# The last image's convolution in a two-layer vision model: where its second batches accumulate in PSUM

## The chip, the cores and the metric

The kernel runs on one core of a Trainium2 chip. The metric is device time in microseconds of one launch: the median of the runs. Three runs of the kernel before gave 10369.3, 10372.5 and 10379.58 us.

The core has TensorE (PE, matrix products into the accumulation memory PSUM), VectorE (DVE), ScalarE (ACT), GpSimd (POOL) and SyncE (SP, which here starts the DMA transfers). PSUM has 8 banks; a bank holds 512 float32 numbers in each of 128 partitions.

## The reference, cut to what matters

Two layers work on four images of 64 x 64 pixels with 128 channels. Layer 0 is attention and a recurrent network; layer 1 is a selective scan and a mixture of experts. The change is in the first part of the selective scan:

```
xz = jnp.einsum('bhwc,ec->bhwe', x, in_proj_w)
xin, z = jnp.split(xz, 2, axis=-1)
xc = jnp.transpose(xin, (0, 3, 1, 2))
xc = lax.conv_general_dilated(xc, conv_w, (1, 1), [(1, 1), (1, 1)],
                              feature_group_count=d, ...)
xc = jax.nn.silu(xc + conv_b[None, :, None, None])
x0 = xc.reshape(B, d, L)
x1 = jnp.transpose(xc, (0, 1, 3, 2)).reshape(B, d, L)
```

So each image is normalised, projected to 256 channels `xin` and 256 gates `z`, and each of the 256 channels is convolved with its own 3 x 3 filter. The result passes through silu and is kept in two orders, by rows (`x0`) and by columns (`x1`), for the scans that follow.

## The kernel before

The program runs attention, then the recurrent network, then `selective_scan`, then `experts`. `selective_scan` calls three functions one after the other: `scan_inputs` (what is shown above, L824), `scans` (L951) and `scan_outputs`. Results pass between them in DRAM. `scans` can begin only when the memory that `scan_inputs` holds has come free.

Inside `scan_inputs` three generators each take an image `b`:
- `centred(b)` (L855) loads the image, subtracts the mean and sums the squares in a PSUM tile with the tag `norm`, which has one bank (L121 writes it, L132 reads it).
- `projected(b)` (L871) scales the image (L145, L148) and, for each of 8 chunks of 512 pixels, makes four products `in_ps` (L880). Each takes one of three banks with the tag `mm`. DVE copies the first two to `xin` (L884), and ACT writes the other two to `z` through silu (L886).
- `convolved(b)` (L890) takes the two halves `h` of 128 channels, and in each half two batches of four chunks, `c0 = 0` and `c0 = 4`. So an image has four batches.

A batch is one PSUM tile with the tag `conv`, of four banks and with one buffer (L895). With `mm` and `norm` this makes 3 + 1 + 4 = 8 banks, all there are. The filter is carried out on PE as nine taps, each a product with a 32 x 32 diagonal matrix. The loops are: tap `n`, chunk `i` of the batch, strip `r` of 32 channels (L896 to L904). Strip `r` of the channels goes to bank `r`, and chunk `i` to partitions `32*i` to `32*i + 31`. That is 9 x 4 x 4 = 144 products, which the profile shows as 288 records, two for each.

Then ACT empties the tile with 16 activations of 32 partitions by 512 numbers (L914), bank by bank, into `u`. After both batches of a half, POOL copies `u` into the order by columns (`uc`, L922), and SP stores both (L927). The first load of `scans` is a constant, `w_x`, at L159.

The driver (L935 to L947) runs `convolved(b)` and, after each of its batches, two steps of `projected(b + 1)` and of `centred(b + 2)`. For the last image, `b = 3`, there is nothing of those two left. The order of instructions in an engine's queue in this stage isn't written out by hand: a scheduler sets it when the program is built, starting from the order of the program and from when tiles come free. In `scans` the order is written out by hand.

Of the kernel before, what the change touches and what calls it, by code (L numbers as in the profile page):

```python
# [19 lines left out]
F32 = mybir.dt.float32  # L20
# [6 lines left out]
P = 128  # L27
B, HW, C = 4, 64, 128
L = HW * HW
CH = 512  # L30
# [18 lines left out]
def chunk(c):  # L49
    return slice(c * CH, (c + 1) * CH)  # L50
# [100 lines left out]
def constant(nc, pool, value, name, shape=(P, 1)):  # L151
    t = pool.tile(list(shape), F32, name=name, tag=name)
    nc.vector.memset(t, value)
    return t


def loaded(nc, pool, src, name):
    t = pool.tile(list(src.shape), F32, name=name, tag=name)
    nc.sync.dma_start(t, src)  # L159
    return t  # L160
# [662 lines left out]
@with_exitstack  # L823
def scan_inputs(ctx, tc, a, x2, us, gates):  # L824

    nc = tc.nc
    cst = ctx.enter_context(tc.tile_pool(name="si_c", bufs=1))
    big = ctx.enter_context(tc.tile_pool(name="si_b", bufs=1))
    work = ctx.enter_context(tc.tile_pool(name="si_w", bufs=2))
    ps = ctx.enter_context(tc.tile_pool(name="si_p", bufs=3, space=PSUM))  # L830

    ident = cst.tile([P, P], F32, name="ident")
    make_identity(nc, ident)
    norms = Norms(nc, cst, ident, C, banks=3)
    eps6 = constant(nc, cst, 1e-6, "eps6")
    w_in = loaded(nc, cst, a["w_in"], "w_in")
    w_conv = loaded(nc, cst, a["w_conv"], "w_conv")
    zeros = constant(nc, cst, 0.0, "zeros", (P, LP - L))
    taps = [(0, 0)] + [
        (dy, dx) for dy in (-1, 0, 1) for dx in (-1, 0, 1) if (dy, dx) != (0, 0)  # L840
    ]


    ident32 = cst.tile([P, 32], F32, name="ident32")
    b_conv = cst.tile([P, ND, 4], F32, name="b_conv")
    for i in range(4):
        rows = slice(32 * i, 32 * i + 32)
        nc.vector.tensor_copy(ident32[rows], ident[rows, rows])
        nc.sync.dma_start(b_conv[rows], a["b_conv"].rearrange("(r j) h -> j h r", j=32))
    diag = cst.tile([P, ND, 9, 32], F32, name="diag")  # L850
    for h in range(ND):
        for n in range(9):
            nc.vector.tensor_scalar_mul(diag[:, h, n, :], ident32, w_conv[:, h, n : n + 1])

    def centred(b):  # L855
        ln = big.tile([P, L], F32, tag="ln", name=f"ln_{b}", bufs=2)
        var = norms.begin(ps, 1)
        for n in range(NCH // 4):
            xs = []
            for c in range(4 * n, 4 * n + 4):  # L860
                x = work.tile([P, CH], F32, tag="x", name="x", bufs=6)
                nc.sync.dma_start(x, x2[b][:, chunk(c)])
                xs.append([x])
            yield
            yield
            norms.centre(ps, work, var, n, xs, [[ln[:, chunk(4 * n + g)]] for g in range(4)])
            yield
            yield
        centres[b] = ln, norms.end(work, var, eps6)

    def projected(b):  # L871
        ln, r = centres[b]
        xin = xins[b] = big.tile([P, ND, L], F32, tag="xin", name=f"xin_{b}", bufs=2)
        for c in range(NCH):
            if c % 4 == 0:
                norms.scale(ps, r, c // 4, [[ln[:, chunk(c + g)]] for g in range(4)])
            z = work.tile([P, ND, CH], F32, tag="z", name="z")
            for h in range(2 * ND):
                pt = ps.tile([P, CH], F32, tag="mm", name="in_ps")
                nc.tensor.matmul(  # L880
                    pt, w_in[:, h * P : (h + 1) * P], ln[:, chunk(c)], start=True, stop=True
                )
                if h < ND:
                    nc.vector.tensor_copy(xin[:, h, chunk(c)], pt)  # L884
                else:
                    nc.scalar.activation(z[:, h - ND, :], pt, AF.Silu)  # L886
            nc.sync.dma_start(gates[b][c], z)
            yield

    def convolved(b):  # L890
        for h in range(ND):
            u = big.tile([P, L], F32, tag="u", name=f"u_{b}", bufs=2)
            image = xins[b][:, h, :].rearrange("p (h w) -> p h w", w=HW)
            for c0 in range(0, NCH, 4):
                pt = ps.tile([P, 4, CH], F32, tag="conv", name="conv_ps", bufs=1)  # L895
                for n, (dy, dx) in enumerate(taps):  # L896
                    left, right = max(0, -dx), min(HW, HW - dx)
                    for i in range(4):
                        first = (c0 + i) * RPC
                        top, end = max(first, -dy), min(first + RPC, HW - dy)  # L900
                        for r in range(4):
                            rows = slice(32 * r, 32 * r + 32)
                            to = pt[32 * i : 32 * i + 32, r, :].rearrange("p (h w) -> p h w", w=HW)
                            nc.tensor.matmul(  # L904
                                to[:, top - first : end - first, left:right],
                                diag[rows, h, 3 * (dy + 1) + dx + 1, :],
                                image[rows, top + dy : end + dy, left + dx : right + dx],
                                start=n == 0,
                                stop=n == len(taps) - 1,
                            )  # L910
                for r in range(4):
                    for i in range(4):
                        rows = slice(32 * i, 32 * i + 32)
                        nc.scalar.activation(  # L914
                            u[32 * r : 32 * r + 32, chunk(c0 + i)],
                            pt[rows, r, :],
                            AF.Silu,
                            bias=b_conv[rows, h, r : r + 1],
                        )
                yield  # L920
            by_columns = big.tile([P, L], F32, tag="uc", name=f"uc_{b}", bufs=2)
            nc.gpsimd.tensor_copy(  # L922
                by_columns.rearrange("p (w h) -> p w h", w=HW),
                u.rearrange("p (h w) -> p w h", w=HW),
            )
            for o, t in enumerate((u, by_columns)):
                nc.sync.dma_start(us[b][o][:, h, :L], t)  # L927
                nc.sync.dma_start(us[b][o][:, h, L:], zeros)

    centres, xins = {}, {}
    for _ in centred(0):
        pass
    for b in range(-1, B):  # L935
        others = [
            step(n)
            for step, n in ((projected, b + 1), (centred, b + 2))
            if n < B
        ]  # L940
        for _ in convolved(b) if b >= 0 else range(ND * NCH // 4):
            for _ in range(2):
                for other in others:
                    next(other, None)
        for other in others:
            for _ in other:
                pass  # L947
# [838 lines left out]
```

## Time and profile before

| | us |
|---|---|
| median of three runs | 10372.5 |
| the profiled execution | 10381.96 |
| its span, first to last instruction | 10379.9 |
| end of `scan_inputs`: last eviction (ACT, L914) ends | 3707.3 |
| first load of `scans` (SP, L159) | 3721.0 |
| end of the stretch with scans, about | 9700 |

The windows view of three stretches (start and end in us from the span's start; then length, busy time and instructions of PE, PE's weight loads, DVE, ACT and POOL, the granted clock of TensorE as a share of full speed, DMA's busy share, GB/s) reads:

```profile
3200.00:3725.00 525.00, 400.62 (x5058) 174.88 (x5058) 108.64 (x174) 242.20 (x364) 60.73 (x13) 0.86 0.30 116
3725.00:9700.00 5975.00, 5558.75 (x77992) 3175.38 (x77992) 5556.60 (x5507) 4161.80 (x7203) 5502.78 (x3458) 0.99 0.57 146
9700.00:10380.00 680.00, 461.96 (x1920) 195.65 (x1920) 416.97 (x545) 110.72 (x177) 2.20 (x3) 0.80 0.49 176
```

The first stretch is `scan_inputs`, 5% of the span. In a profile's lines `L904` is a line of the kernel, `conv_ps<-xin,diag` names what is written and what is read, `x288` is a count, and a bracket at the end of a timeline's line gives the idle time before it and the work that ended it.

### The profile page before, as it was taken

The numbers are of one execution on the slowest core, as the hardware profiler recorded it, in microseconds if no ns is written. First come the engines' busy times: TensorE is split into PE (matmuls) and PEld (weight loads), VectorE is DVE, ScalarE is ACT, GpSimd is POOL, SyncE is SP. The second block draws the span as 40 slices with busy tenths as digits, with TensorE's granted clock in tenths as the row PEclk, the third lists the DMA queues.
The fourth block names the chain that finished last, engine by engine and source line by source line (L and its number), as shares of the span: only waits on it lengthen the run. The fifth ranks groups of instructions, "written<-read, shape, count | busy, mean of one in ns | idle before, by whom it ended". The sixth has DMA issues, their size and how long they took to land.

```text
span 10379.9 us, 244130 instructions
## 1 busy us (share of the span) xinstructions
PE 9318.5 (90%) x103920; PEld 4400.3 (42%) x103920; DVE 8856.0 (85%) x8023; ACT 6815.2 (66%) x9682; POOL 5616.8 (54%) x3513
## 2 busy tenths in 40 slices
PE   7999999999888869999999999999999999999766
PEld 3222222222233335555555555555555555555323
DVE  7999999999685159999999999999999999999864
ACT  3778777777564557777776776776777766767311
POOL 0000000000011159999999999999999999999300
PEclk8999999999999979999999999999999999999877
DMA  4000000000212335555655565655565555566634
GB/s 181 7 7 31 9 31 7 9 7 8 86 61 93 125 118 139 144 153 149 154 146 139 143 158 148 151 146 136 144 158 153 144 141 144 146 149 157 203 131 167
DMA packets 529249, 1173.61 MB, mean 113 GB/s; under 512 B 47954, under 2 KB 436634, under 8 KB 498330
## 3 DMA queue, kind: packets, MB, share of 16 engines
q1 hardware_dynamic: 528154, 1157.87, 40.1%
q8 instruction: 827, 13.55, 0.5%
q14 instruction: 268, 2.20, 0.1%
HBM read 816.74 MB, written 190.00 MB: 97 GB/s over the span
## 4 chain that ended last, share of the span: by engine, by line
DVE 49%; issue 8%; PE 4%; DMA 2%; DVEq 1%; POOL 0%; ACT 0%; SPq 0%; POOLq 0%; ACTq 0%
DVE states L1255 41%; DVE db L1248 3%; DVE b_diag L1139 1%; DVE log L1111 1%; PE db L1217 1%; DMA weights<-in_w 1%; PE y L1308 1%; DVEq L1255 0%; DVE y L1446 0%; PE norm_mean_ps L115 0%; PE x_ps L1065 0%; DVEq L1248 0%; PE gate_ps L1536 0%; PE pool_ps L1566 0%; PE norm_var L121 0%
## 5 line engine op out<-in xcount | busy, mean ns | idle before, releaser
L1255 DVE TENSOR_TENSOR_SCAN states<-decays,db 128x920 f32<-128x920 f32 x2304 | 4761.9, 2067 | 175.9 <-DVE db L1248 4.6
L1279 POOL TENSOR_TENSOR products<-states,c_ring 128x912 f32<-128x912 f32 x2304 | 4513.7, 1976 | 437.7 <-DVE db L1248 167.8
L1193 ACT ACTIVATE decays<-dt,a_logs 128x456 f32<-128x456 f32 x4608 | 3100.2, 676 | 97.6
L1217 PEld LDWEIGHTS db<-b_diag,dtu_t 32*128 32x128 f32 x18432 | 2233.7, 187 | 1790.5 <-issue 1332.6
L1217 PE MATMUL db<-b_diag,dtu_t 32*128 32x128 f32 x18432 | 2636.8, 282 | 374.4 <-DVE states L1255 308.7
L1217 PE MATMUL db<-b_other,dtu_t 32*128 32x128 f32 x18432 | 2674.5, 284 | 5.6 <-DMA b_other<-b_diag 3.1
L1226 PE MATMUL y<-zeros 32*128 32x128 f32 x17224 | 2496.4, 283 | 5.4 <-issue 5.3
L1308 PE MATMUL y<-products,ident 64*64 64x456 f32 x18432 | 2314.2, 570 | 9.4 <-issue 7.0
L1217 PEld LDWEIGHTS db<-b_other,dtu_t 32*128 32x128 f32 x18432 | 2236.3, 187 | 8.6 <-issue 4.7
L1226 PEld LDWEIGHTS y<-zeros 32*128 32x128 f32 x17224 | 2085.4, 187 | 7.4 <-issue 7.3
L333 DVE TENSOR_TENSOR total<-total,ring 128x2048 f32<-128x2048 f32 x768 | 1759.3, 2291 | 76.0 <-ACT ring L301 10.4
masks.py:197 POOL MEMSET ident<- 128x128 f32 x6 | 1.2, 205 | 3154.3 <-SPq L177 2840.7
L301 ACT ACTIVATE ring<-sa 128x2048 f32<-128x2048 f32 x640 | 1203.7, 1881 | 467.3 <-PE sa L286 467.3
L1266 ACT COPY carry<-states 128x8 f32<-128x8 f32 x576 | 117.7, 204 | 1677.6 <-DVE states L1255 1627.0
L310 PE MATMUL av<-ring,v_at 128*32 128x512 f32 x8192 | 1010.0, 599 | 0.1
L286 PE MATMUL sa<-q_at,k_at 32*128 32x512 f32 x5120 | 731.8, 641 | 61.2 <-ACT ring L301 36.1
L301 ACT ACTIVATE ring<-sb 128x1536 f32<-128x1536 f32 x512 | 741.4, 1448 | 0.0
L1308 PEld LDWEIGHTS y<-products,ident 64*64 64x64 f32 x18432 | 493.3, 131 | 334.5 <-issue 54.9
L286 PE MATMUL sb<-q_at,k_at 32*128 32x512 f32 x3072 | 555.3, 615 | 50.7 <-ACT ring L301 50.7
L310 PEld LDWEIGHTS av<-ring,v_at 128*32 128x32 f32 x8192 | 210.4, 109 | 700.9 <-issue 676.3
L1248 DVE COPY db<-states 128x8 f32<-128x8 f32 x1728 | 302.9, 175 | 205.8 <-PE db L1217 25.2
L286 PEld LDWEIGHTS sa<-q_at,k_at 32*128 32x128 f32 x5120 | 200.3, 183 | 616.7 <-ACT ring L301 310.0
(208 smaller groups left out, 9178.6 us busy)
## 6 DMA issues: line engine op xcount, KB each, us to landing
c_ring<-c_rows SPq DMA_DIRECT2D x576, 912.0 KB, 7.5
b_other<-b_diag SPq DMA_DIRECT2D x288, 512.0 KB, 9.6
u<-u_r SPq DMA_DIRECT2D x72, 456.0 KB, 10.4
y_r<-sum SPq DMA_DIRECT2D x72, 456.0 KB, 4.3
u<-u_c SPq DMA_DIRECT2D x72, 456.0 KB, 10.4
y_c<-sum SPq DMA_DIRECT2D x72, 456.0 KB, 4.7
weights<-in_w SPq DMA_DIRECT2D x32, 1024.0 KB, 12.9
x<-x SPq DMA_DIRECT2D x96, 256.0 KB, 2.7
```

The costliest lines, as they stand in the source:

```text
L286: nc.tensor.matmul(s[:, m, :], k[rows, tokens(t)], q[rows, chunk(chunk_state["c"])], start=True, stop=True,)
L301: nc.scalar.activation(ring[:, lo : lo + n, :], s[:, at : at + n, :], AF.Exp)
L310: nc.tensor.matmul(chunk_state["av"][rows, :], chunk_state["v"][:, t, rows], ring[:, at + i, :], start=t == 0, stop=t == NJ - 1,)
L333: nc.vector.tensor_add(total, total, w)
L1193: nc.scalar.activation(to, dt, AF.Exp, scale=scale)
L1217: nc.tensor.matmul(bank.rearrange("p (n t) -> p n t", n=4)[:, :, at : at + 32], v.dtu[rows, h, s, :], b[rows, s, 4 * self.q : 4 * self.q + ...
L1226: nc.tensor.matmul(y[:, idle // 2, :P], zeros[rows], zeros[rows], start=False, stop=False)
L1248: nc.vector.tensor_copy(self.edge(self.db[:, SKIP:], v.into), self.edge(before.slot(states), v.outof) if self.nth else self.carry(),)
L1255: nc.vector.tensor_tensor_scan(order(self.slot(states)), order(self.slot(decays, 1 if self.v.back else 0)), order(self.db[:, SKIP:][:, : 2 ...
L1266: nc.scalar.copy(self.carry(), self.edge(self.slot(states), self.v.outof))
L1279: nc.gpsimd.tensor_mul(to, h, c)
L1308: nc.tensor.matmul(to, ident[rows, rows], of, start=begins, stop=ends)
```

## The change

For the last image only, and in its batches with `c0 = 4` only, the batch no longer takes the four-bank `conv` tile. It takes four tiles of one bank: three with the tag `mm` and one with the tag `norm`. All other batches keep the `conv` tile, now addressed as a list of its four banks. The products, the activations and their order in the program stay the same.

```diff
             for c0 in range(0, NCH, 4):
-                pt = ps.tile([P, 4, CH], F32, tag="conv", name="conv_ps", bufs=1)
+                if b == B - 1 and c0:
+
+                    pt = [ps.tile([P, CH], F32, tag="mm", name="conv_ps") for _ in range(3)]
+                    pt.append(ps.tile([P, CH], F32, tag="norm", name="conv_ps", bufs=1))
+                else:
+                    pt = ps.tile([P, 4, CH], F32, tag="conv", name="conv_ps", bufs=1)
+                    pt = [pt[:, r, :] for r in range(4)]
...
-                            to = pt[32 * i : 32 * i + 32, r, :].rearrange("p (h w) -> p h w", w=HW)
+                            to = pt[r][32 * i : 32 * i + 32, :].rearrange("p (h w) -> p h w", w=HW)
...
-                            pt[rows, r, :],
+                            pt[r][rows, :],
```

## The prediction

> **What bounds the kernel now.** I began with the page's chain of work that ended last, to see whether the stage touched by the change is on it at all. Most of that chain is VectorE's scan, L1255, a later stage. So I asked for the chain inside the window 3560 to 3725 us, where the convolution of the last image ends; columns are start, duration, what.
>
> ```profile
> 3706.65 0.69 ACT u L914
> 3707.34 0.03 POOLq L922
> ...
> 3707.45 7.09 POOL uc L922
> ...
> 3714.56 6.27 DMA u_c<-uc
> ...
> 3721.02 0.33 SPq L159
> ...
> 3724.21 5.30 DMA u<-u_r
> ```
>
> The reader should see that nothing lies beside this path. The last eviction of the convolution (ACT, L914) releases the transposing copy on POOL, that releases the store, and only when the store has landed does SyncE load the constants of the scans. Whatever moves the last eviction moves the start of the scans, and the 5975 us after it, by the same amount.
>
> Then the timeline of 3612 to 3710 us, PE and ACT lines of the last image's four batches (start, duration, engine, work, and the idle time before it with its releaser):
>
> ```profile
> 3612.06 1.91 PE L904 MATMUL conv_ps<-xin,diag 32*32 32x512 f32 x2 [2.91 <-ACT u L914]
> 3613.90 2.08 PE L880 MATMUL in_ps<-ln,w_in 128*128 128x512 f32 x2
> 3615.90 10.67 PE L904 MATMUL conv_ps<-xin,diag 32*32 32x512 f32 x286
> 3637.78 11.54 PE L904 MATMUL conv_ps<-xin,diag 32*32 32x512 f32 x288 [11.20 <-ACT u L914]
> 3660.54 12.15 PE L904 MATMUL conv_ps<-xin,diag 32*32 32x512 f32 x288 [11.22 <-ACT u L914]
> 3683.89 12.28 PE L904 MATMUL conv_ps<-xin,diag 32*32 32x512 f32 x288 [11.20 <-ACT u L914]
> ...
> 3626.66 11.06 ACT L914 ACTIVATE u<-conv_ps,b_conv 32x512 f32<-32x512 f32 x16 [10.05 <-PE conv_ps L904]
> 3649.43 11.06 ACT L914 ACTIVATE u<-conv_ps,b_conv 32x512 f32<-32x512 f32 x16 [11.70 <-PE conv_ps L904]
> 3672.78 11.06 ACT L914 ACTIVATE u<-conv_ps,b_conv 32x512 f32<-32x512 f32 x16 [12.29 <-issue]
> 3696.27 11.06 ACT L914 ACTIVATE u<-conv_ps,b_conv 32x512 f32<-32x512 f32 x16 [12.44 <-PE conv_ps L904]
> ```
>
> This is a strict alternation: PE fills the one four-bank tile, ACT empties it with 16 activations, PE waits 11.2 us, three times over. For earlier images projections and norms fill part of such a wait (L880 and L145 stand in it at 3575 to 3584 us); for the last image nothing is left to do.
>
> Third, the windows view on PE inside the second batch (window, its length, PE busy and records, granted clock, DMA share, GB/s):
>
> ```profile
> 3637.70:3640.00 2.30, 2.23 (x48) 0.50 0.00 0
> 3640.00:3643.00 3.00, 3.00 (x73) 0.65 0.02 5
> 3643.00:3646.00 3.00, 3.00 (x106) 1.00 0.00 0
> 3646.00:3649.50 3.50, 3.32 (x105) 1.00 0.02 5
> ```
>
> Each wait also costs PE its clock: half speed at first, full after some 5 us. Where b=2's last batch followed other PE work (3591.26 us), its 286 records took 9.58 us, at clock 1.00 in the windows view, against 11.5 to 12.3 here.
>
> **What the Trainium skill says.** "PSUM — Partial Sum Buffer", section on bank collisions, has two engines run clean at once on different banks, and raise an error on the same bank and 32-partition quadrant. So TensorE may write the mm and norm banks while ScalarE reads the conv banks. The trace agrees as far as it goes: projections write mm banks at 3600.77 us while 16 evictions of conv banks take 11.06 us, as without company. "TensorE: Matmul & The Clock Gate", section "What's actually happening", gives half clock after an idle window of about 3.4 us and full clock after about as long a busy one; the 0.50 then 1.00 above agrees. "TensorEngine Tiling (Array Packing)", "Key Properties", says that a change of tiling mode drains TensorE; the one convolution matmul that stands alone between projections (3612.06 to 3613.90) took 1.84 us. "ScalarE: Activation LUTs", "What ACT_TABLE_LOAD costs", prices an activation with a pointer bias at 280 ns + 0.833 ns per element, neighbours overlapping by 93 ns: 613 ns of pitch for 512 elements. The trace has 11.06/16 = 691 ns, which I use.
>
> **The change, part by part.** Of the last image's four batches, the second and the fourth (c0 = 4, for h = 0 and 1) get four one-bank tiles, three with tag mm and one with tag norm. The matmuls and activations are the same in number, shape and operands. No DMA is added, and none is moved past another on SP.
>
> Are the banks free? The last user of the norm bank is activation L132 at 3508.5 us, and nothing takes it again. The last user of an mm bank is the z activation at 3616.01 + 0.60 us. Batch 2 on PE is due at 3626.6, when batch 1 ends. So its waits have ended 10 us earlier.
>
> New sequence, with the first batch unmoved (PE 3612.06 to 3626.6, ACT from 3626.66):
> - PE batch 2 follows at 3626.6 at full clock. 288 records at 9.58/286 us are 9.65 us, so it ends at 3636.2. ACT batch 1 ends at 3626.66 + 11.06 = 3637.72 and goes straight on to batch 2.
> - PE batch 3 needs the conv tile, free at 3637.72, and ends near 3647.4; ACT batch 2 ends at 3648.8.
> - PE batch 4 needs the mm and norm banks, free at 3648.8, and ends near 3658.5; ACT batch 3 ends at 3659.9.
> - ACT is now the bound: 4 x 11.06 = 44.24 us without a gap, from 3626.66 to 3670.90.
>
> Before it ended at 3696.27 + 11.06 = 3707.33. The gain is 36.43 us: the three gaps in ACT, (3649.43 - 3637.72) + (3672.78 - 3660.49) + (3696.27 - 3683.84) = 11.71 + 12.29 + 12.43. About 33.6 of it is the waits of PE, the rest the clock.
>
> The cover is thin: PE has about 1.4 us in hand per batch. Bounds: at the speed of today's slowest batch (12.28 us), each of three batches would make ACT wait for 12.28 - 11.06 = 1.2 us, and 32.8 us would remain. Above, nothing can be gained over 36.4 by this part, because the first batch's end and ACT's work stay. I take 36.4: a pause of 1.5 us between batches is shorter than those after which the trace shows 0.50.
>
> Separate tiles let a bank be handed over after 4 of 16 activations. In the order of the loop the first four matmuls touch all four banks, so that gives nothing in batch 4; each activation's extra check for its tile finds the matmuls done. I take 0; the bounds are a gain of at most the 1.4 us in hand that ACT can't use, so 0, and a loss of about 0.05 us (the issue gaps seen) x 32, under 2 us.
>
> Reordering is the unknown. PE's queue isn't the program's order: a convolution matmul stands ahead of the last projection at 3612.06. The norm bank is free from 3508.5, so matmuls of batch 2's strip r = 3 could likewise be put into earlier gaps as soon as the image's chunks 4 to 7 are projected (3579 to 3608 us). Gaps are there: 1.85 us before 3586.72, 2.91 us before 3612.06. I expect a few, at no cost; each that fits no gap costs up to 1.84 us.
>
> POOL's copy (7.09), the store (6.27) and SP's loads follow as before, 36.4 us earlier. The h = 0 copy and store (today from 3660.6) come at 3648.8 to 3662, done before those of h = 1 begin at 3671. Nothing of another timing becomes late: the next waits are the same constants' loads.
>
> Sum: the profiled execution took 10381.96 us (span 10379.9), so such a one would take 10345.5. The median of the runs shown, 10372.5, lies 9.5 below the profiled time; 10372.5 - 36.4 = **10336**.
>
> **The rivals.**
> - *PE keeps a low clock.* For it: batches follow with pauses. Against: today's full clock within 5 us. At 60 records in 3.0 us of half clock (third batch's start) a batch takes 288 x 50 ns = 14.4 us, 3.3 over ACT's 11.06, three times: 10 us back, 10346.
> - *The gain is given back later.* The scan stage has one hole where chain and DMA meet: c_ring 11.29 and u 12.44 us at 6492.8 to 6516.5. A second of that kind costs about 24 us: 10360. Losing this one gives 10312. For it: the scans start at another moment. Against: one such hole in nearly 6000 us.
> - *Matmuls get ordered bank by bank.* Then one row strip works at a time; four column tiles at the projections' pitch (4.56/10 us) give 0.114 us a record, 32.8 us a batch, 21.7 over ACT, in two batches: 43 - 36 gives 10379, no change. Against: all four banks of batch 2 are free long before it.
> - *Slower.* Strip r = 3 of batch 2 (9 taps x 4 = 36 matmuls, norm bank) is scattered between projections and batches of image 2, each breaking PE's tiling mode at 1.84 us: 66 us, and 10372.5 - 36.4 + 66 = 10402. It decides from 20 lone matmuls outside idle gaps (36.4/1.84), and from 31 for over 0.2%. For it: the pair at 3612.06. Against: only a few gaps lie between 3579 and 3612.
>
> **How the numbers follow.** Forecast 0.78, low clock 0.05, hole gone 0.02: faster, 0.85. Given back 0.06, bank by bank 0.04: the same, 0.10. Scattered 0.05: slower. A change of 0.2% (21 us) is about what measurement tells from none. The forecast's own range is 10326 to 10347, from the runs' spread (10369.3 to 10379.6) and the bounds 32.8 and 36.4. To leave out no more than 2 in 10 I take 10322 to 10358.
>
> **What would show it.** ACT's L914 in four stretches of 11.06 us without gaps; the wait of PE's L904 for L914 in this window down from 36.5 to some 3 us; batches near 9.7 us; POOL's last copy at about 3671; scans from there on as before. It is wrong if ACT shows gaps over 2 us between batches, or L904 appears in many pieces between L880's.

## The result and the profile after

The changed kernel takes 10338.63 us (median of 13 runs, 10332.18 to 10356.69); the kernel before took 10369.3 in the 13 runs beside them. The ratio is 0.9969 with a 95% interval of 0.9961 to 0.9976, a gain of 25 to 40 us. The profiled execution went from a span of 10379.9 us to 10343.5.

In the profile after, lines below L895 stand six higher: the convolution's matmuls are L910, the evictions L920, the copy by columns L928. The timeline of ScalarE in the last image, with the last batch of image 2 at 3593.93 (start, duration, engine, work, count, idle time before and its releaser):

```profile
3593.93 11.04 ACT L920 ACTIVATE u<-conv_ps,b_conv 32x512 f32<-32x512 f32 x16 [9.48 <-PE conv_ps L910]
...
3620.64 22.16 ACT L920 ACTIVATE u<-conv_ps,b_conv 32x512 f32<-32x512 f32 x32 [11.26 <-PE conv_ps L910]
3642.97 22.11 ACT L920 ACTIVATE u<-conv_ps,b_conv 32x512 f32<-32x512 f32 x32 [0.17 <-issue]
```

The 64 evictions of the last image now stand in two rows of 32 with 0.17 us between them, where there were four of 16 with gaps of 11.7 to 12.4 us. From the first to the end of the last it is 3642.97 + 22.11 - 3620.64 = **44.44 us**; before it was 3707.33 - 3626.66 = 80.67. I call this the local time. The change took 36.23 us from it.

TensorE's timeline over the same stretch:

```profile
3593.75 4.56 PE L880 MATMUL in_ps<-ln,w_in 128*128 128x512 f32 x10
3598.24 1.05 PE L910 MATMUL conv_ps<-xin,diag 32*32 32x512 f32 x4
3599.22 1.13 PE L880 MATMUL in_ps<-ln,w_in 128*128 128x512 f32 x2
3600.27 1.04 PE L910 MATMUL conv_ps<-xin,diag 32*32 32x512 f32 x4
3601.24 1.12 PE L880 MATMUL in_ps<-ln,w_in 128*128 128x512 f32 x2
3602.30 1.91 PE L910 MATMUL conv_ps<-xin,diag 32*32 32x504 f32 x16
3605.02 1.71 PE L910 MATMUL conv_ps<-xin,diag 32*32 32x512 f32 x2 [0.82 <-ACT u L920]
...
3608.67 20.51 PE L910 MATMUL conv_ps<-xin,diag 32*32 32x512 f32 x548
3631.74 18.74 PE L910 MATMUL conv_ps<-xin,diag 32*32 32x512 f32 x524 [2.56 <-ACT u L920]
3651.57 2.16 PE L910 MATMUL conv_ps<-xin,diag 32*32 32x512 f32 x52 [1.09 <-issue]
```

From 3608.67 on, batches run into each other: TensorE waits 2.56 us for ScalarE once, and then goes through two batches without a stop for it. (The break of 1.09 us near the end was no wait for ScalarE; breaks of its kind come up again below.) The view of waits says the same in two lines, before (window 3612 to 3710 us) and after (3612 to 3700 us); columns are the total, how often, the longest:

```profile
PE conv_ps L904 <- ACT u L914: 36.5, 4, 11.2
ACT u L914 <- PE conv_ps L904: 34.2, 3, 12.4
```

```profile
ACT u L920 <- PE conv_ps L910: 11.3, 1, 11.3
...
PE conv_ps L910 <- ACT u L920: 2.6, 1, 2.6
```

TensorE's wait for ScalarE fell from 36.5 us to 2.6, and ScalarE's for TensorE from 34.2 to 11.3; what is left is the wait for the first batch. The chain of waits after is the old one, earlier (SPq is SyncE starting a transfer):

```profile
3664.39 0.69 ACT u L920
...
3665.19 7.07 POOL uc L928
...
3672.28 6.26 DMA u_c<-uc
...
3678.73 0.33 SPq L159
```

Eviction, POOL's copy, the store, the first load of the scans: no other work has become the last to arrive.

### The profile page after: what moved, and what is told of

Read it like the earlier page. It is cut to its first block, busy times and chain, and to the rows that moved or that the text cites. A ratio compares the mean times of both kernels' runs of the same rounds, so it can differ in the third digit from the quotient of the medians.

```text
span 10343.5 us, 244132 instructions
## 1 busy us (share of the span) xinstructions
PE 9317.0 (90%) x103920; PEld 4399.6 (43%) x103920; DVE 8855.7 (86%) x8023; ACT 6813.5 (66%) x9682; POOL 5613.8 (54%) x3513
## 4 chain that ended last, share of the span: by engine, by line
DVE 49%; issue 8%; PE 3%; DMA 2%; DVEq 1%; POOL 0%; ACT 0%; SPq 0%; POOLq 0%; ACTq 0%
DVE states L1261 42%; DVE db L1254 3%; DVE b_diag L1145 1%; DVE log L1117 1%; PE db L1223 1%; DVEq L1261 0%; PE norm_mean_ps L115 0%; DMA weights<-in_w 0%; PE y L1314 0%; DVE y L1452 0%; DVEq L1254 0%; PE pool_ps L1572 0%; POOL products L1285 0%; PE gate_ps L1542 0%; DMA x<-x_back 0%
## 5 line engine op out<-in xcount | busy, mean ns | idle before, releaser
L1223 PEld LDWEIGHTS db<-b_other,dtu_t 32*128 32x128 f32 x18432 | 2239.4, 187 | 11.3 <-DMA b_other<-b_diag 5.9
```

The costliest lines, as they stand in the source:

```text
L1223: nc.tensor.matmul(bank.rearrange("p (n t) -> p n t", n=4)[:, :, at : at + 32], v.dtu[rows, h, s, :], b[rows, s, 4 * self.q : 4 * self.q + ...
```

## Where the whole gain went

The stage can be bounded by two loads that every kernel here has: `w_in` at its start and `w_x` right after it. From SyncE's timelines, before and then after:

```profile
3206.93 0.33 SPq L159 DMA_DIRECT2D w_in<-in_w_in  x1
```

```profile
3721.02 0.33 SPq L159 DMA_DIRECT2D w_x<-in_w_x  x1
```

```profile
3200.78 0.33 SPq L159 DMA_DIRECT2D w_in<-in_w_in  x1
```

```profile
3678.73 0.33 SPq L159 DMA_DIRECT2D w_x<-in_w_x  x1
```

The stage took 3721.02 - 3206.93 = 514.09 us and now takes 477.95, a gain of 36.14. It began 6.15 us earlier in the second trace, although nothing ahead of it is changed, and the rest of the program gave 5.9 us back: 10379.9 - 3721.02 = 6658.9 us before, 10343.5 - 3678.73 = 6664.8 after. So the span's 36.4 agrees with the stage only because these two cancel.

Most of the 5.9 us lies in the scans. The windows view of the changed kernel shows two stretches of them that follow each other (busy time and count of PE, weight loads, DVE, ACT, POOL; granted clock; DMA share; GB/s):

```profile
8045.00:8062.00 17.00, 17.00 (x140) 8.54 (x132) 10.78 (x11) 7.08 (x12) 12.44 (x9) 0.57 0.19 65
8062.00:8080.00 18.00, 18.00 (x253) 10.41 (x253) 16.32 (x18) 9.86 (x18) 14.47 (x11) 1.00 0.45 108
```

In the first, TensorE's clock is at 0.57 and VectorE, which should be working without a break here, is busy 63% of the time; in the second, at full clock, 91%. The trace's clock records have four such halvings in the scans of the changed kernel, 54.6 us in all, and five of 37.5 us in all in the kernel before. Whether that is the change's doing is asked below.

## The experiments

All numbers called local time are from the first eviction of the last image to the end of its last eviction or copy.

**One half at a time.** The change joins three seams between batches at once. Two kernels join some of them:

```diff
-                if b == B - 1 and c0:
+                if b == B - 1 and c0 and h == 0:
```

> Only the second batch of the first half (h = 0) takes the mm and norm banks; the fourth batch is as in the kernel before. Theory (each seam between two batches gives the gap that ScalarE had there): the seams 1-2 and 2-3 close, 3-4 stays. From the start of the first eviction of the last image to the end of its last one 80.7 - 11.7 - 12.3 = 56.7 us (before 80.7, after 44.4); whole kernel 24 us less than before. Rival (the gain is mainly one effect, such as the clock of TensorE or the order of the queue, that is there as soon as one batch moves): nearly the whole 36 us, or next to nothing.

ScalarE's timeline:

```profile
3622.93 33.24 ACT L920 ACTIVATE u<-conv_ps,b_conv 32x512 f32<-32x512 f32 x48 [12.13 <-PE conv_ps L910]
3668.60 11.06 ACT L920 ACTIVATE u<-conv_ps,b_conv 32x512 f32<-32x512 f32 x16 [12.44 <-PE conv_ps L910]
```

Three batches stand in one row of 48 and the fourth after a gap of 12.44 us. Local time 3668.60 + 11.06 - 3622.93 = 56.73 us, 23.94 less than before; stage 488.0; ratio 0.9978 (0.9968 to 0.9988). The other one, with `h == 1`:

> Only the fourth batch (h = 1) takes the mm and norm banks. Theory: only the seam 3-4 closes; first eviction to last 80.7 - 12.4 = 68.3 us, whole kernel 12 us less than before. With the run of the other half it must add up to the whole change, 36.4. Rival: as there, nearly all or next to nothing.

```profile
3624.04 11.06 ACT L920 ACTIVATE u<-conv_ps,b_conv 32x512 f32<-32x512 f32 x16 [10.29 <-PE conv_ps L910]
3646.59 11.06 ACT L920 ACTIVATE u<-conv_ps,b_conv 32x512 f32<-32x512 f32 x16 [11.49 <-PE conv_ps L910]
3669.83 22.13 ACT L920 ACTIVATE u<-conv_ps,b_conv 32x512 f32<-32x512 f32 x32 [12.18 <-issue]
```

Here only the last two stand together: 67.92 us, 12.75 less. Stage 500.8; ratio 0.9993 (0.9984 to 1.0001), which alone would tell nothing. The two gains make 36.7 us, against 36.2 for the whole. Each half gives the gaps of its own seams, and the rival of one effect for all of them is out.

The first of these kernels also shows the clock after a short wait and after a long one, as it holds a batch of each kind. TensorE's timeline and its windows view (length, busy and records, clock, DMA share, GB/s):

```profile
3634.05 9.67 PE L910 MATMUL conv_ps<-xin,diag 32*32 32x512 f32 x288 [1.48 <-ACT u L920]
3656.22 12.28 PE L910 MATMUL conv_ps<-xin,diag 32*32 32x512 f32 x288 [12.51 <-ACT u L920]
```

```profile
3634.00:3644.00 10.00, 9.67 (x288) 1.00 0.02 5
3656.00:3662.00 6.00, 5.78 (x99) 0.50 0.31 132
3662.00:3668.50 6.50, 6.50 (x205) 0.98 0.02 5
```

After a wait of 1.48 us a batch takes 9.67 us; after 12.5 us of waiting it takes 12.28, the first 6 us of it at half clock. ScalarE's gaps of 11.7 to 12.4 us are therefore mostly the batch itself on TensorE, at the low speed that came with the wait.

**The changed kernel again.**

> The changed kernel itself, unaltered, beside the next three on one chip. Theory (the local gain is fixed, the rest of a run's difference comes from short halvings of TensorE's clock in the scans, in other places in each execution): first eviction of the last image to its last one 44.4 us again, within 0.5, while the total gain differs from 36.4 by up to 10 us and the halvings lie elsewhere than in the first trace of this kernel. Rival (the scans have become slower through the change): the halvings lie in the same places, and the scans' stretch is again some 7 us longer than in the kernel before.

```profile
3632.40 44.29 ACT L920 ACTIVATE u<-conv_ps,b_conv 32x512 f32<-32x512 f32 x64 [11.97 <-PE conv_ps L910]
```

Local time 44.3 us, stage 479.7, ratio 0.9962 (0.9948 to 0.9975). From the load of `w_x` to the last copy of sums, the scans took 5977.9 us in the kernel before, 5983.2 in the first trace of the changed one and 5975.9 in this one; the kernels with half the change took 5974.1 and 5963.2. So the scans did not become slower through it. Their halvings lasted 31 us in this trace. I had expected them elsewhere, and that is only partly so: two of five lie within 9 us of earlier ones (6648 and 8048 us, where the first trace had 6640 and 8043), the others don't. Over all 13 traces of this document the scans' time goes with the halved time: 5962 us where 10.2 us were halved (the wide eviction below), 5981 and 5987 in the two where 58.0 were (bank by bank, and strip 0 alone), a correlation of 0.94. That fits the halvings as the cause of these differences; no run changed the clock alone.

**The order of the matmuls.** Two kernels make the strip the outer loop in the two batches concerned. Bank by bank:

```diff
-                for n, (dy, dx) in enumerate(taps):
+                alone = b == B - 1 and c0
+                for turn in range(4 * len(taps) if alone else len(taps)):
+                    n, strips = (turn % 9, [turn // 9]) if alone else (turn, range(4))
+                    dy, dx = taps[n]
...
-                        for r in range(4):
+                        for r in strips:
```

> As the changed kernel, but in the second and fourth batch of the last image the strip r is the outermost loop, so that one bank is filled after the other. Theory: only four of sixteen array tiles work at a time, about 0.114 us a record, 32.8 us a batch in place of 9.7; ScalarE's evictions hide behind it. First eviction to last: 32.8 + 9.7 + 32.8 + 2.8 = 78 us, about the kernel before. Rival: the records are bound by issue and not by the tiles in use, so the order does not matter: 44 us, and a bank handed over early would even gain.

It was worse than theory and rival alike: local time 98.3 us, 10402.49 in all, ratio 1.0020 (1.0010 to 1.0031). ScalarE's timeline, with some of its groups left out, and TensorE's windows:

```profile
3627.20 13.84 ACT L923 ACTIVATE u<-conv_ps,b_conv 32x512 f32<-32x512 f32 x20 [11.22 <-PE conv_ps L913]
3647.82 2.76 ACT L923 ACTIVATE u<-conv_ps,b_conv 32x512 f32<-32x512 f32 x4 [6.78 <-PE conv_ps L913]
3659.67 2.75 ACT L923 ACTIVATE u<-conv_ps,b_conv 32x512 f32<-32x512 f32 x4 [9.10 <-PE conv_ps L913]
...
3722.75 2.75 ACT L923 ACTIVATE u<-conv_ps,b_conv 32x512 f32<-32x512 f32 x4 [9.09 <-PE conv_ps L913]
```

```profile
3627.00:3632.00 5.00, 5.00 (x55) 1.00 0.02 3
...
3647.00:3659.00 12.00, 12.00 (x80) 0.50 0.00 0
...
3690.00:3702.00 12.00, 12.00 (x76) 0.50 0.00 0
```

The banks of the second batch arrive 11.85 us apart (3647.82 to 3659.67). TensorE's records leave no idle time, and still the clock stands at 0.50 through 12 us in both batches; in the third batch between them, which works all four strips, it was back at 1.00 (3667 to 3671 us). I had priced such a batch from a pitch at full clock. To see whether one strip at work is the reason, the same with two strips at a time (`[k, k + 1]`, k = 0 and then 2):

> As the bank-by-bank kernel, but the second and fourth batch of the last image go through two strips at a time (r = 0 and 1, then 2 and 3). What is open from the bank-by-bank run: its local time was 98.3 us and not the 78 worked out, with a granted clock of 0.50 while TensorE's records show no idle time. Theory (one strip at work is too little for the full clock): two strips work eight array tiles, about 0.057 us a record, 16.4 us a batch at full clock; if the clock stays full, first eviction to last about 16.4 + 9.7 + 16.4 + 5.5 = 48 us; if it halves here too, 80 us or so. Rival (the halving was chance, as those in the scans): a halving of not over 20 us in one of the two batches.

```profile
3630.00:3640.00 10.00, 10.00 (x201) 1.00 0.01 3
3655.00:3665.00 10.00, 10.00 (x217) 1.00 0.71 294
```

The clock stays full and the local time is 45.3 us, in the one run of this kernel. So it was one strip alone that went with the half clock, in both batches of one run. One strip is also one bank here, and the two were not taken apart. The loop's order, which the change kept, is worth 54 us of local time here (98.3 against 44.4).

**What bounds the stage after the change.** ScalarE's activations read 32 of 128 partitions. Read as a whole bank, a batch takes 4 in place of 16, and VectorE must place the four chunks:

```diff
+                    if b == B - 1:
+                        wide = work.tile([P, CH], F32, tag="x", name="wide", bufs=6)
+                        nc.scalar.activation(
+                            wide, pt[r], AF.Silu, bias=b_conv[:, h, r : r + 1]
+                        )
+                        for i in range(4):
+                            nc.vector.tensor_copy(
+                                u[32 * r : 32 * r + 32, chunk(c0 + i)],
+                                wide[32 * i : 32 * i + 32, :],
+                            )
+                        continue
```

> As the changed kernel, but the last image's evictions read a whole bank (128 partitions by 512, 4 activations a batch and not 16) into a work tile, and VectorE copies the four chunks to their places (16 copies of 32 by 512). Theory (after the change ScalarE's 64 activations of 0.69 us are the bound): with 2.8 us a batch on ScalarE the bound passes to TensorE, 3 x 9.7 = 29 us after the first batch, plus 2.8 and the last copies; if a copy takes 0.35 us, first eviction to last copy about 33 to 36 us in place of 44.4, 8 to 11 us gained on the changed kernel. If a copy takes 0.69 us as one of 128 by 512 out of PSUM does, VectorE is as slow as ScalarE was: 45 us and no gain. Rival (TensorE or the hand-over of banks is already the bound): no gain whatever the copies take.

The tile view of the work tile (duration in ns: least, median, greatest) and the timelines of ScalarE, VectorE and POOL:

```profile
L924 DVE COPY u<-wide x64: 415/419/5469, 3625.6 to 3662.4; 32x512 f32<-32x512 f32 x64
L920 ACT ACTIVATE wide<-conv_ps,b_conv x16: 678/687/697, 3624.8 to 3653.9; 128x512 f32<-128x512 f32 x16
```

```profile
3624.80 2.42 ACT L920 ACTIVATE wide<-conv_ps,b_conv 128x512 f32<-128x512 f32 x4 [11.20 <-PE conv_ps L910]
...
3652.15 2.42 ACT L920 ACTIVATE wide<-conv_ps,b_conv 128x512 f32<-128x512 f32 x4 [6.61 <-issue]
```

```profile
3634.44 6.95 DVE L924 COPY u<-wide 32x512 f32<-32x512 f32 x16 [1.91 <-ACT wide L920]
3643.90 18.89 DVE L924 COPY u<-wide 32x512 f32<-32x512 f32 x32 [2.51 <-issue]
```

```profile
3641.51 7.58 POOL L939 COPY uc<-u 128x4096 f32<-128x4096 f32 x1 [24.84 <-DVE u L924]
```

An activation on 128 partitions takes 687 ns, on 32 it took 679. ScalarE's part is 2.4 us a batch, batches on TensorE follow every 8.9 to 9.4 us, and the bound has passed to TensorE as the theory had it. Local time 38.0 us, 6.4 less than in the changed kernel, but 2 to 5 more than expected: the copies take 0.43 us each, 16 in 6.95 us, except that the third and fourth batch's 32 took 18.89. One copy took 5.47 us, while POOL's copy by columns ran (3641.51 to 3649.09). "SBUF — State Buffer", section "Who interferes with whom" of the Trainium skill says that VectorE in a two-port mode and GpSimd exclude each other for a whole instruction; the slow copy ended at 3649.37, 0.28 us after POOL's, which agrees, though no run shows in which mode it went. The stage took 473.8 us. In all: 10335.36 us, ratio 0.9961 (0.9947 to 0.9974), not to be told from the changed kernel.

With only strips 0 and 1 done so (`if b == B - 1 and r < 2`), the copies should no longer matter:

> Last image only: strips 0 and 1 of each batch are evicted as whole banks and placed by VectorE (8 copies of 0.43 us), strips 2 and 3 go directly as in the changed kernel (8 activations of 0.69 us). Theory (TensorE is the bound, and what is left is the tail): ScalarE 1.2 + 5.5 = 6.7 us and VectorE 3.5 us a batch, both under TensorE's 9.3; GpSimd's copy, in which VectorE stood still for 5 us with all strips placed by it, is covered. First eviction to last 3 x 9.3 + 6.7 = 35 us, 3 less than with all strips placed by VectorE (38.0), 10 less than the changed kernel. Rival (VectorE's standstill still counts): 38 us or more.

It missed: 37.6 us, ratio 0.9956 (0.9943 to 0.9970). VectorE's copies fitted, but the fourth batch took TensorE 12.5 us and not 9.3, with breaks of 1.83 and 0.71 us that the profile puts down to nothing ("issue"). A transfer of 16,384 bytes on the queue that the profile calls "instruction" had landed 1.45 and 1.48 us before TensorE went on. So TensorE probably stood waiting for its own instructions; the last section has the count, and no run tests it.

**All images.** The same two evictions for images 0 to 2 too. Whole banks first, with `if True` in place of `if b == B - 1`:

> All four images evicted as whole banks (4 activations a batch) and placed by VectorE; banks as in the changed kernel. Theory: for images 0 to 2 ScalarE's 11.06 us hold the one conv tile while TensorE, after the projections, waits for it 2 to 3 us a batch and projections wait for z activations queued behind them; with 2.4 us that goes, 2 to 5 us for each of 12 batches, 24 to 60 us besides what the last image gives: about 10270 to 10310. Rival: VectorE (7 us of copies a batch, with GpSimd's copies in their way, and the projections' own copies queued behind) takes ScalarE's place as what holds up TensorE: no gain on images 0 to 2, or a loss, 10330 to 10360.

The stage took 467.9 us, 5.9 less than with the last image alone, and 10338.63 in all, 0.9969 (0.9957 to 0.9981). The rival is nearer: little was gained on images 0 to 2. With strips 0 and 1 only (`if r < 2`):

> As the mixed eviction, for all four images. Theory: ScalarE holds the conv tile 6.7 us and not 11.06, so most of the 2 to 3 us of wait a batch goes: 12 x 2 to 4 = 24 to 48 us besides the last image's 10: 10280 to 10305. Rival: copies of VectorE in the way of the projections: no gain on images 0 to 2, 10328.

ScalarE is now done 6.8 us after a batch (1.27 for two whole banks and 5.52 for eight pieces). The stage took 454.6 us, 25 less than in the changed kernel beside it, and 10317.84 in all, 0.9948 (0.9934 to 0.9961). That is between the theory (10280 to 10305) and the rival (10328), so the theory promised too much. About 20 of the 25 us came on images 0 to 2: from the stage's first load to the first eviction of the last image it was 401.5 us, and 421.8 in the changed kernel beside it. The last image gave less than it could, as its fourth batch came 14.6 us after the third, with two breaks of the kind just named (1.92 and 1.04 us). Again:

> The mixed eviction for all four images once more (strips 0 and 1 as whole banks, placed by VectorE). From the first load of this stage to the first load of the scans 454.6 us were seen, 25 less than in the changed kernel's second trace (479.7). Theory: 455 again within 3, and 10315 to 10322 in all. Rival (its lead over the changed kernel, 10317.8 to 10331.7 with intervals that overlap, was chance): 10330 or more.

Stage 457.7, 10322.8 us, 0.9950 (0.9936 to 0.9964), so the stage is as expected and the whole time just above the range given. In the stage this version beats the wide eviction, and the changed kernel by 20 us or more, both times. In whole time its intervals still overlap with the changed kernel's, so there it is likely and not shown. With strip 0 alone (`if r < 1`):

> As the mixed eviction of all images, but only strip 0 goes as a whole bank: ScalarE 0.6 + 8.3 = 8.9 us a batch, VectorE 1.7. Theory: on the last image TensorE (9.3) is still the bound, so little changes there but a tail of 8.9 and not 6.7; on images 0 to 2 the conv tile comes free 2.2 us later than in the mixed one and is waited for again: 5 to 15 us slower than the mixed one, stage 460 to 470. Rival (VectorE's copies are what holds images 0 to 2 back): faster than the mixed one.

The stage took 455.5 us, the time was 10324.67, 0.9947 (0.9933 to 0.9961): no slower than with two strips. The theory missed: the conv tile coming free 2.2 us later wasn't felt on images 0 to 2, which took 402.0 us to the last image's first eviction.

## Why the prediction was right

- *The path.* The last eviction sets the start of the scans: the chain after is the same chain, and the stage's 36.14 us show in full at the load of `w_x`.
- *The banks.* They were free in time; TensorE's first matmuls of the second batch waited for no bank.
- *The gain.* 36.43 us were forecast from three gaps, 36.23 came in the profile, and seam by seam 23.94 and 12.75 where the gaps gave 24.0 and 12.4.
- *The cover.* TensorE's batch was put at 9.65 us with 1.4 in hand. It took 9.67 in the trace that isolates it. TensorE's wait in the window fell to 2.6 where some 3 was forecast, but that the totals agree is partly luck: two pauses of about 1.5 us were forecast, and one of 2.56 came, as part of the second batch had been done ahead. After it the clock stood at 0.50 for 3.4 us (3632.6 to 3636.0), which was not forecast, and the third batch took 10.5 us, which left no second pause. This stayed inside the 1.4 us in hand. In the second trace the two pauses were there, 1.18 and 1.06 us, and the clock stayed at 1.00. The lower bound, 32.8 for batches at low clock, wasn't needed.
- *Reordering.* It happened and cost nothing, as forecast: 26 records (13 matmuls) of the second batch's norm bank stand at 3574.37 to 3604 us in four pieces among the projections. From the projections' start to the next convolution it was 3605.02 - 3593.75 = 11.27 us, and before 3612.06 - 3600.77 = 11.29. The price of 1.84 us for a lone piece was one at half clock (0.50 from 3612 to 3614 us before); at full clock a piece of two matmuls stood 0.98 us (3598.24 to 3599.22).
- *The sum.* 10336 forecast, 10338.63 measured. That they lie 2.6 us apart is partly luck: the medians differ by 30.7 us, 5.7 less than forecast, from a kernel before that stood 3.2 lower than the base of the sum. Both are within the spread. The ratio that 36.4 us make, 0.9965, lies in the interval. The forecast time of POOL's last copy, 3671 us, was 6 late, because the stage itself began earlier.
- *The rivals.* No hole was added in the scans, the clock came up, and nothing was put in order bank by bank. The hole that two rivals were priced from was misread, though: the chain ran through two DMA transfers from 6492.8 to 6516.5 us, but VectorE was busy for 28.23 of the 30 us from 6490 to 6520, and TensorE for 27.45, so nothing stood still there. After the change these transfers are not in the chain, and the scans gained no 24 us by it. The price of the order bank by bank was wrong too: "0.114 us a record, 32.8 us a batch" gave 10379 and no change. The run gave 10402 and slower, since the pitch taken was one at full clock and a lone strip ran at half: 72 records of a bank took 11.85 us, 0.165 each.

## What to carry to other kernels

Where two engines take turns on one buffer and an earlier phase's buffers lie idle by then, the gain of lending them is read as the gaps of the engine that will be the bound, not as the waits of the other: here 36.4 us of gaps on ScalarE, against 33.6 of waits on TensorE, since TensorE was also slower after the waits. A gain of a third of a per cent is better checked between two fixed events of the stage than in the whole time, where it stands beside a spread of 30 us (10361 to 10392 in 13 runs of the kernel before). After such a change, count what the new bound does per batch: an activation over a quarter of the partitions costs as much as one over all.

## What the runs showed of the hardware

- One strip of array tiles at work left TensorE's clock at 0.50 for 12 us and more with no idle time in its records; two strips kept it at 1.00. "TensorE: Matmul & The Clock Gate" of the Trainium skill, section "What's actually happening", ties half clock to idle windows. The measurement differs: in this run the clock was at half while TensorE was at work without idle time.
- In the scans, with TensorE over 90% busy, the clock halves for 3 to 17 us a few times in an execution, from 10.2 us in all (the wide eviction of the last image) to 58.0 (bank by bank, and strip 0 alone). VectorE fell behind in the one shown above, busy 63% of the time against 91% after it.
- An activation of 128 x 512 took 687 ns and one of 32 x 512 took 679.
- TensorE's breaks of over 0.5 us that the profile puts down to "issue", in the convolutions between 3550 and 3720 us, are 21 in the 13 traces. Each ended 1.22 to 1.58 us after a transfer of 16,384 bytes on the queue called "instruction" had landed. That points to waits for instructions and is not tested.
